# State-space scan: the entering states written beside B instead of into the scan's buffer

## The chip, the cores and the metric

The kernel runs on one core of one Trainium2 chip. The metric is the device time of one execution in microseconds (us). Engines are called as in the profile: PE (matrix products), DVE and POOL (elementwise work), ACT (activations and copies), SP (issues DMAs). Each engine works through its own queue in order; semaphores tie the queues together.

## The reference, cut to what matters

Two layers, each with a residual. The first is neighbourhood attention (7 x 7) on two images of 48 x 48 tokens with 768 channels. The second is a bidirectional selective scan over L = 2304 tokens, with 1536 inner channels d and 16 states n for each channel:

```python
def step(h, inp):
    d_t, B_t, C_t, u_t = inp
    dA = jnp.exp(d_t[..., None] * A)
    h = dA * h + (d_t * u_t)[..., None] * B_t[:, None, :]
    y = jnp.einsum('bdn,bn->bd', h, C_t)
    return (h, y)
```

`d_t` is delta (a softplus), `B_t` and `C_t` are rows of a small projection. The scan is run forward and backward with separate weights, `x * Dp` is added, the result is gated and projected, and everything is in fp32.

## The kernel before, in words

**Tiling.** Channels lie on partitions: 12 blocks `k` of 128. Time is cut into 6 chunks of `CL` = 384 tokens. A *pass* is one image, one direction and one chunk (24 passes); a *unit* is one channel block of a pass (288 units). A unit has four *groups* `g` of `SG` = 4 states, so there are 1152 groups. Within a chunk the recurrence over tokens is one instruction for two states: `tensor_tensor_scan` (line 1252) on a row of `W = CL + 2` = 386 cells per state.

**The two extra cells.** In the buffer `hb` of a group each state has 386 cells: 384 for the chunk, one ahead and one behind. The cell at the entering end holds the state that the previous chunk left; the one at the other end separates it from the next state. The decay tile `da` has fixed values, one and zero, in those two cells, set at the start of a pass direction (line 1188).

**One group** (`group` in `scan`) goes through these steps:
- `first` fills `hb`. It writes the eight end cells (the *edge fill*, lines 1216 or 1220), then the product of delta u and B over the 384 tokens of four states (line 1224). It runs whole on DVE or whole on POOL. On POOL it reads delta u from SBUF (`dus`), on DVE from a PSUM copy `du` that ACT makes once per unit (line 1193). `was` is the pair of state columns that go into the ends, or zeros in the first chunk.
- `step` on ACT makes exp(delta A), one instruction per state (line 1241), into one of two PSUM tiles `da`, each for two states.
- `two_steps` on DVE is the scan (line 1252).
- POOL multiplies by C (line 1267), ACT keeps the leaving state in `state` (line 1275), PE adds the states up by transposes (line 1284).

**Per three units** `deltas_of` loads `u` (line 1131 issues this load and that of the delta weights), makes delta on PE and ACT (lines 1142, 1148, 1153), `vt` = u Dp on ACT (line 1161), and delta u in place of `u` on POOL (line 1166).

**Per pass** `chunk` loads B and C, spread over all partitions, as four tiles each, `bc0` to `bc3` and `bc4` to `bc7` (line 1373). Each of the eight has one buffer, so a new chunk's load waits for the last reader of the old one.

**What sets the order.** Nothing is issued in source order. All work is handed to a planner (`Order`), with a price in ns, a key (the unit at which it is due), what it reads and writes, and sometimes an alternative engine (`alt`: three of the four groups may have `first` on the other engine). The planner plays the queues through with these prices and takes, for the engine that can start soonest, the work that is ready; with `early=EARLY` a work goes ahead of others that are ready then. It fixes the order in each queue once, and the program is built so. It also fills long waits of PE with transposes that change nothing (`idle`, line 1482). Beside the scans it places the rest: the first layer's attention of image 1, the input and output projections. Attention of image 0 comes ahead of all scans.

Of the kernel before, what the change touches and what calls it, by code (L numbers as in the profile page):

```python
# [16 lines left out]
P = 128  # L17
# [228 lines left out]
def tile_kernel(  # L246
# [34 lines left out]
    ]  # L281
    zero = res.tile([P, SG, 2], F32, tag="zero", name="zero")
    nc.gpsimd.memset(zero, 0.0)

    ones = wk.tile([1, CL], F32, tag="yt", name="ones", bufs=1)
    nc.gpsimd.memset(ones, 1.0)
# [32 lines left out]
    def sb(tag, shape, n, parts=1):  # L319
        return Buf(f"{tag}_{n}", wk, shape, tag, BUFS.get(tag, 1), parts)  # L320
# [26 lines left out]
    def act(n, pointers=0):  # L347
        return 60 + 90 * pointers + n * 0.833

    def dve(n):  # L350
        return 55 + n * 1.042

    def rows_of(t, k0, n, l0, cl):
        return t[k0 * P : (k0 + n) * P, l0 : l0 + cl].rearrange("(k p) l -> p k l", p=P)
# [768 lines left out]
    def deltas_of(ch, k0, x):  # L1123

        q, b, back, l0, cl, dt = (ch[v] for v in ("q", "b", "back", "l0", "cl", "dt"))
        c, at, n = slice(0, cl), x - 1.0, f"{ch['s']}_{k0}"
        u, w = sb("u", [P, KB, CL], n, KB), sb("dtw", [RK + 1, KB * P], n)
        dl = sb("dlt", [P, KB, CL], n, KB)

        def fetch():  # L1130
            nc.sync.dma_start(u[:, :, c], rows_of(us[back][b], k0, KB, l0, cl))
            nc.sync.dma_start(w.ap, q["dtT"][:, k0 * P : (k0 + KB) * P])

        add(
            "SP", 800, fetch, at - 0.7, r=[(us[back][b], cols(l0, cl, k0, KB))], w=[u, w],
            size=P * KB * (cl + RK) * 4,
        )
        for j in range(KB):
            acc = ps("mm", f"dl_{n}_{j}")
            add(  # L1140
                "PE", mm(1, cl),
                lambda j=j, acc=acc: nc.tensor.matmul(
                    acc[:, c], w[:, j * P : (j + 1) * P], dt[:, c], start=True, stop=True
                ),
                at + 0.01 * j, r=[dt, w, u], w=[acc, (dl, j)], early=EARLY,
            )
            add(
                "ACT", act(cl), lambda j=j, acc=acc: nc.scalar.copy(dl[:, j, c], acc[:, c]),
                at + 0.01 * j, [acc], [(dl, j)], early=EARLY,
            )  # L1150

        def softplus():
            nc.scalar.activation(dl[:, :, c], dl[:, :, c], AF.Softplus)
            nc.scalar.preload_act_table_set("natural_log_exp_and_others")

        add("ACT", 2600 + 120 + act(KB * cl), softplus, at + 0.05, [dl], [dl], early=EARLY)
        vts = [sb("vt", [P, CL], f"{n}_{j}") for j in range(KB)]
        for j in range(KB):
            add(
                "ACT", act(cl, 1) + 40,  # L1160
                lambda j=j: nc.scalar.mul(vts[j][:, c], u[:, j, c], q["Dp"][:, k0 + j : k0 + j + 1]),
                at + 0.03 + 0.25 * j, [(u, j)], [vts[j]], early=EARLY,
            )
            add(
                "POOL", 960,
                lambda j=j: nc.gpsimd.tensor_mul(u[:, j, c], dl[:, j, c], u[:, j, c]), at + 0.06 + 0.25 * j,  # L1166
                [(dl, j), (u, j)], [(u, j)], early=EARLY,
            )
        return [((dl, j), (u, j), vts[j]) for j in range(KB)]

    def scan(ch, k, x, dlj, duj, vt):
# [11 lines left out]
        if k == 0 and ch["first"]:  # L1183
# [6 lines left out]
                add("DVE", 200, turn, x - 0.1, w=[da])  # L1190
        du = ps("du", n)
        add(
            "ACT", act(cl), lambda: nc.scalar.copy(du[:, c], dus[:, ju, c]), x - 0.5, [duj], [du],
            early=EARLY,
        )

# [5 lines left out]
        def group(g):  # L1202
            m = f"{n}_{g}"
            now = at + 0.25 * g
            hb = sb("hb", [P, SG * W], m, SG + 1)
            body = (hb, range(SG))
            of = (slice(None), k, slice(g * SG, (g + 1) * SG))
            was = zero if ch["first"] else state[of][:, :, 0:2] if back else state[of][:, :, 1:3]

            def first():
                around = cells(hb, SG)[:, :, ends]
                if filled.eng == "POOL":
                    by, on = dus[:, ju, c], nc.gpsimd
                    on.tensor_copy(around, was)
                else:

                    by, on = du[:, c], nc.vector
                    on.scalar_tensor_tensor(  # L1220
                        around, du[:, : 2 * SG].rearrange("p (j e) -> p j e", e=2), 0.0, was, ALU.mult,
                        ALU.add,
                    )
                on.tensor_mul(  # L1224
                    cells(hb, SG)[:, :, h], by.unsqueeze(1).to_broadcast([P, SG, cl]), bc[g][:, :, c]
                )

            on = {"DVE": dve(SG * cl) + 75, "POOL": SG * cl * 2.2 + 140}
            main, other = ("DVE", "POOL") if g in (0, 1) else ("POOL", "DVE")
            filled = add(  # L1230
                main, on[main], first, now - (0.35 if main == "POOL" else 0.1),
                [du, duj, bc[g], (state, k * NSG + g)], [hb], after=marks.get(marks["n"] - 6),
                alt=(other, on[other]) if g in (1, 2, 3) else None,
            )

            def step(j):
                i = g * SG + j
                da = das[j // 2 % 2]
                add(
                    "ACT", act(cl, 1) + 45,  # L1240
                    lambda: nc.scalar.activation(  # L1241
                        cells(da, 2)[:, j % 2, h], dl[:, jd, c], AF.Exp, scale=q["A"][:, k, i : i + 1]
                    ),
                    now + 0.06 * j - 0.06, [dlj], [(da, j % 2)], due=True,
                )

            def two_steps(j):
                da = das[j // 2 % 2]
                at2 = (slice(None), slice(j * W, (j + 2) * W))
                mark = add(  # L1250
                    "DVE", (4 * W + 42) / 0.96,
                    lambda: nc.vector.tensor_tensor_scan(  # L1252
                        flip(hb[at2]), flip(da[:, : 2 * W]), flip(hb[at2]), 0.0, ALU.mult, ALU.add
                    ),
                    now + 0.06 * j, [da], [(hb, (j, j + 1, SG))],
                )
                marks[marks["n"]] = mark
                marks["n"] += 1

            for j in range(0, SG, 2):  # L1260
                step(j)
                step(j + 1)
                two_steps(j)

            add(
                "POOL", SG * cl * 2.03 + 10,
                lambda: nc.gpsimd.tensor_mul(  # L1267
                    cells(hb, SG)[:, :, h], cells(hb, SG)[:, :, h], bc[NSG + g][:, :, c]
                ),
                now + 0.25, [body, bc[NSG + g]], [body],  # L1270
            )
            if not ch["final"]:
                add(
                    "ACT", 90,
                    lambda: nc.scalar.copy(
                        state[of][:, :, 1:2], cells(hb, SG)[:, :, leaves : leaves + 1]
                    ),
                    now + 0.3, [body, (hb, SG)], [(state, k * NSG + g)],
                )

            def add_up():
                for j in range(SG):
                    for t in range(nt):
                        nc.tensor.matmul(  # L1284
                            py[:tp, t * P : (t + 1) * P], cells(hb, SG)[:, j, h][:, tb[t]], ident,
                            start=False,
                            stop=g == NSG - 1 and j == SG - 1 and t == nt - 1,
                            is_transpose=True, skip_group_check=True,
                        )

            add(
                "PE", SG * nt * 109 + 60, add_up, now + 0.45, [body, py], [py],
                opens=False if g == NSG - 1 else None,
            )
# [62 lines left out]
    def chunk(b, back, i, at):  # L1357
# [8 lines left out]
        )  # L1366
        bc = []
        for g in (0, 1, 2, NSG, 3, NSG + 1, NSG + 2, NSG + 3):
            t = sb(f"bc{g}", [P, SG, CL], s)
            r = RK + 1 + g * SG  # L1370
            add(
                "SP", 400,
                lambda t=t, r=r: nc.sync.dma_start(
                    t[:, :, :cl], src[r : r + SG, l0 : l0 + cl].partition_broadcast(P)
                ),
                at - 1 + 0.25 * (g % NSG) + 0.3 * (g >= NSG), [(src, cols(l0, cl))], [t],
                size=P * SG * cl * 4,
            )
            bc.append((g, t))
# [153 lines left out]
```

## Time and profile before

| what | value |
|---|---|
| time, median of 3 runs | 7284.69 us (7281.98 to 7290.29) |
| the profiled execution | 7284.3 us, its span 7282.5 us |
| DVE busy | 6207.4 us (85%) |
| POOL busy | 5628.0 us (77%) |
| ACT busy | 4924.7 us (68%) |
| PE busy | 6429.7 us (88%), of it fillers (L1482) 608.8 us |
| scans (L1252) | 2304, mean 1747 ns |
| `first` on DVE (L1224) / on POOL | 674, mean 1758 ns / 478, mean 3455 ns |
| product with C on POOL (L1267) | 1152, mean 3186 ns |
| exponentials (L1241) | 4608, mean 584 ns |
| edge fill on DVE (L1220) / on POOL (L1216) | 674, median 143 ns / 478, median 198 ns |
| state copy on ACT (L1275) | 960, mean 189 ns |

A line such as "L1252 DVE" is one source line on one engine. A wait is the time that an engine stood idle ahead of an instruction, put down to the instruction that released it. The name of a tile stands without buffer number, and `hb<-du,bc` means that `hb` is written from `du` and `bc`. [...]

### The profile page before, as it was taken

The numbers are of one execution on the slowest core, as the hardware profiler recorded it, in microseconds if no ns is written. First come the engines' busy times: TensorE is split into PE (matmuls) and PEld (weight loads), VectorE is DVE, ScalarE is ACT, GpSimd is POOL, SyncE is SP. The second block draws the span as 40 slices with busy tenths as digits, with TensorE's granted clock in tenths as the row PEclk, the third lists the DMA queues.
The fourth block names the chain that finished last, engine by engine and source line by source line (L and its number), as shares of the span: only waits on it lengthen the run. The fifth ranks groups of instructions, "written<-read, shape, count | busy, mean of one in ns | idle before, by whom it ended". The sixth has DMA issues, their size and how long they took to land.

```text
span 7282.5 us, 105644 instructions
## 1 busy us (share of the span) xinstructions
PE 6429.7 (88%) x38214; PEld 4891.8 (67%) x38214; DVE 6207.4 (85%) x7016; ACT 4924.7 (68%) x9948; POOL 5628.0 (77%) x2411
## 2 busy tenths in 40 slices
PE   7999988888899899899888888888888888889888
PEld 4555556666667766666666666666677887777777
DVE  1353449999888999888999999999999999999998
ACT  1232248788776787767888777778776666777764
POOL 0000009999988999869788899999999999999997
PEclk9999999999999999999999999999999999999999
DMA  6565453554556454554443542343466676555543
GB/s 180 169 198 154 138 162 102 157 151 127 153 163 189 137 158 137 157 166 135 134 144 94 157 141 91 100 133 110 132 178 188 170 204 201 181 165 170 168 147 107
DMA packets 1326322, 1101.03 MB, mean 151 GB/s; under 512 B 134168, under 2 KB 1316040, under 8 KB 1325768
## 3 DMA queue, kind: packets, MB, share of 16 engines
q1 hardware_dynamic: 1325800, 1094.27, 50.1%
q8 instruction: 303, 4.96, 0.3%
q14 instruction: 219, 1.79, 0.1%
HBM read 881.11 MB, written 213.57 MB: 150 GB/s over the span
## 4 chain that ended last, share of the span: by engine, by line
DVE 35%; PE 23%; POOL 15%; ACT 13%; issue 9%; DMA 4%; SPq 1%; DVEq 0%; POOLq 0%; ACTq 0%
DVE hb L1252 24%; POOL hb L1267 10%; POOL hb L1224 5%; DVE hb L1224 5%; PE mm_qk L382 5%; ACT da L1241 4%; DVE uz_u L931 3%; PE py L1284 3%; PE mm_v L382 2%; PE mm_ao L382 2%; PE mm_xin L382 1%; PE mm_z L382 1%; PE da L821 1%; ACT uz_u L924 1%; PE mm_out L382 1%
## 5 line engine op out<-in xcount | busy, mean ns | idle before, releaser
L1252 DVE TENSOR_TENSOR_SCAN hb<-da,hb 128x772 f32<-128x772 f32 x2304 | 3924.0, 1747 | 182.7 <-ACT da L1241 140.1
L1267 POOL TENSOR_TENSOR hb<-hb,bc 128x1536 f32<-128x1536 f32 x1152 | 3651.7, 3186 | 342.1 <-DVE hb L1252 286.0
L1241 ACT ACTIVATE da<-dlt,A 128x384 f32<-128x384 f32 x4608 | 2675.9, 584 | 1169.9 <-DVE hb L1252 1098.3
L1284 PE MATMUL py<-ident,hb 128*128 128x128 f32 x13824 | 1761.3, 281 | 263.8 <-POOL hb L1267 261.2
L1284 PEld LDWEIGHTS py<-ident,hb 128*128 128x128 f32 x13824 | 1591.2, 145 | 473.0 <-POOL hb L1267 366.7
L1224 POOL TENSOR_TENSOR hb<-u,bc 128x1536 f32<-128x1536 f32 x478 | 1651.7, 3455 | 38.6
L1224 DVE TENSOR_TENSOR hb<-du,bc 128x1536 f32<-128x1536 f32 x674 | 1184.7, 1758 | 23.0
L1166 POOL TENSOR_TENSOR u<-dlt,u 128x384 f32<-128x384 f32 x288 | 289.6, 1007 | 532.0 <-DMA bc<-xdf 412.9
L382 PE MATMUL mm_z<-xc,w_z 128*128 128x384 f32 x1728 | 609.9, 493 | 13.5 <-ACT uz_z L951 9.4
L1482 PE MATMUL py<-ident 128*128 128x128 f32 x4926 | 608.8, 278 | 0.0
L382 PE MATMUL mm_xin<-xc,w_x 128*128 128x390 f32 x1656 | 588.8, 498 | 21.3 <-DVE uz_u L931 8.5
L1482 PEld LDWEIGHTS py<-ident 128*128 128x128 f32 x4926 | 563.5, 143 | 25.2 <-issue 23.7
L382 PE MATMUL mm_out<-stage_y,w_o 128*128 128x192 f32 x3168 | 550.6, 331 | 15.2 <-DVE xr L1074 7.3
L382 PEld LDWEIGHTS mm_out<-stage_y,w_o 128*128 128x128 f32 x3168 | 522.1, 193 | 34.1 <-DVE xr L1074 9.3
L897 POOL MEMSET xc<- 128x18 f32 x4 | 0.5, 116 | 671.0 <-DMA dlt_qk<-in_w_qkv 671.0
L382 PEld LDWEIGHTS mm_xin<-xc,w_x 128*128 128x128 f32 x1656 | 309.3, 192 | 238.5 <-issue 23.4
L382 PEld LDWEIGHTS mm_z<-xc,w_z 128*128 128x128 f32 x1728 | 319.4, 192 | 220.6 <-ACT uz_z L951 16.5
L931 DVE SCALAR_TENSOR_TENSOR uz_u<-mm_xin,conv_w,uz_u 128x384 f32<-128x384 f32 x792 | 428.0, 607 | 36.0 <-ACT uz_u L924 32.8
L382 PE MATMUL mm_qk<-xc_xn,w_qk 128*128 128x384 f32 x1080 | 384.2, 501 | 11.7 <-ACT pT L828 2.9
L1300 PE MATMUL py<-ident,vt 128*128 128x128 f32 x864 | 160.4, 297 | 230.4 <-ACT yt L1310 230.1
L787 ACT ACTIVATE pr<-pr,sm 128x308 f32<-128x308 f32 x432 | 234.4, 543 | 134.7 <-DVE sm L781 134.2
L1300 PEld LDWEIGHTS py<-ident,vt 128*128 128x128 f32 x864 | 103.1, 148 | 295.0 <-ACT yt L1310 278.5
(171 smaller groups left out, 7043.4 us busy)
## 6 DMA issues: line engine op xcount, KB each, us to landing
w_o<-in_w_opT SPq DMA_DIRECT2D x264, 384.0 KB
bc<-xdf SPq DMA_DIRECT2D x96, 768.0 KB
bc<-xdb SPq DMA_DIRECT2D x96, 768.0 KB
w_x<-in_w_inT SPq DMA_DIRECT2D x144, 384.0 KB
w_z<-in_w_inT SPq DMA_DIRECT2D x144, 384.0 KB
w_qk<-in_w_qkv SPq DMA_DIRECT2D x108, 384.0 KB
u<-uf SPq DMA_DIRECT2D x48, 576.0 KB
sz<-uz_z SPq DMA_DIRECT2D x48, 576.0 KB
```

Of the source, the lines that this page charges most:

```text
L382: nc.tensor.matmul(acc[:m, o0 : o0 + cl], wb[:, wi, wo : wo + m], xb[:, xi, xo : xo + cl], start=c == 0, stop=c == n - 1,)
L787: nc.scalar.activation(pr[j].ap, pr[j].ap, AF.Exp, bias=sm[:, j : j + 1], scale=-1.0, accum_out=sm[:, 2 + j : 3 + j],)
L821: nc.tensor.transpose(bank(pt, 512 - P)[:nk, k * P : (k + 1) * P], pr[j][:, c0 : c0 + nk], ident,)
L931: nc.vector.scalar_tensor_tensor(u, px[:, at[j] : at[j] + cl], q["conv_w"][:, k, j : j + 1], u, ALU.mult, ALU.add,)
L1166: lambda j=j: nc.gpsimd.tensor_mul(u[:, j, c], dl[:, j, c], u[:, j, c]), at + 0.06 + 0.25 * j,
L1224: on.tensor_mul(cells(hb, SG)[:, :, h], by.unsqueeze(1).to_broadcast([P, SG, cl]), bc[g][:, :, c])
L1241: lambda: nc.scalar.activation(cells(da, 2)[:, j % 2, h], dl[:, jd, c], AF.Exp, scale=q["A"][:, k, i : i + 1]),
L1252: lambda: nc.vector.tensor_tensor_scan(flip(hb[at2]), flip(da[:, : 2 * W]), flip(hb[at2]), 0.0, ALU.mult, ALU.add),
L1267: lambda: nc.gpsimd.tensor_mul(cells(hb, SG)[:, :, h], cells(hb, SG)[:, :, h], bc[NSG + g][:, :, c]),
L1284: nc.tensor.matmul(py[:tp, t * P : (t + 1) * P], cells(hb, SG)[:, j, h][:, tb[t]], ident, start=False, stop=g == NSG - 1 and j == SG - 1 a ...
L1300: nc.tensor.matmul(py[:tp, t * P : (t + 1) * P], vt[:, tb[t]], ident, start=t == 0, stop=False, is_transpose=True, skip_group_check=True,)
L1482: nc.tensor.matmul(marks["py"][:, CL : CL + P], ident, ident, start=False, stop=False, is_transpose=True, skip_group_check=True,)
```

## The change

The edge fill of `first` goes. Instead:
- the tiles `bc0` to `bc3` get two more columns for each state, one ahead of B's 384 and one behind (`[P, SG, CL + 2]`); the load writes the middle, with rows of 1536 B now 4 B off the tile's start;
- for each group of a unit ACT copies the state pair `was` into those two columns (976 copies of 128 x 8 elements; in the first chunk of a direction only at `k == 0`, where they are zeros for the whole chunk);
- `u` also gets a column ahead and one behind; ACT writes ones into them once per load (96 copies), and delta u is made between them; `du` is copied with both;
- `first` is one product over 4 x 386 cells: one times state at the ends, delta u times B between.

The product with C, the scans, the exponentials and `bc4` to `bc7` stay. The planner's prices for `first` change from `dve(SG * cl) + 75` to `dve(SG * W)` on DVE and from `SG * cl * 2.2 + 140` to `SG * W * 2.2 + 20` on POOL, and all work is planned anew.

```diff
+    one = res.tile([P, KB, 2], F32, tag="one", name="one")
+    nc.gpsimd.memset(one, 1.0)
...
-        u, w = sb("u", [P, KB, CL], n, KB), sb("dtw", [RK + 1, KB * P], n)
+        u, w = sb("u", [P, KB, CL + 2], n, KB), sb("dtw", [RK + 1, KB * P], n)
...
-            nc.sync.dma_start(u[:, :, c], rows_of(us[back][b], k0, KB, l0, cl))
+            nc.sync.dma_start(u[:, :, h], rows_of(us[back][b], k0, KB, l0, cl))
...
+        add(
+            "ACT", 100, lambda: nc.scalar.copy(u[:, :, :: cl + 1], one), at - 0.3, w=[u], early=EARLY,
+        )
...
-                lambda j=j: nc.gpsimd.tensor_mul(u[:, j, c], dl[:, j, c], u[:, j, c]), at + 0.06 + 0.25 * j,
+                lambda j=j: nc.gpsimd.tensor_mul(u[:, j, h], dl[:, j, c], u[:, j, h]), at + 0.06 + 0.25 * j,
...
-            "ACT", act(cl), lambda: nc.scalar.copy(du[:, c], dus[:, ju, c]), x - 0.5, [duj], [du],
+            "ACT", act(cl), lambda: nc.scalar.copy(du[:, :W], dus[:, ju, :]), x - 0.5, [duj], [du],
...
-                around = cells(hb, SG)[:, :, ends]
-                if filled.eng == "POOL":
-                    by, on = dus[:, ju, c], nc.gpsimd
-                    on.tensor_copy(around, was)
-                else:
-
-                    by, on = du[:, c], nc.vector
-                    on.scalar_tensor_tensor(
-                        around, du[:, : 2 * SG].rearrange("p (j e) -> p j e", e=2), 0.0, was, ALU.mult,
-                        ALU.add,
-                    )
+                by, on = (dus[:, ju, :], nc.gpsimd) if filled.eng == "POOL" else (du[:, :W], nc.vector)
                 on.tensor_mul(
-                    cells(hb, SG)[:, :, h], by.unsqueeze(1).to_broadcast([P, SG, cl]), bc[g][:, :, c]
-                )
-
-            on = {"DVE": dve(SG * cl) + 75, "POOL": SG * cl * 2.2 + 140}
+                    cells(hb, SG), by.unsqueeze(1).to_broadcast([P, SG, W]), bc[g].ap
+                )
+
+            if k == 0 or not ch["first"]:
+                add(
+                    "ACT", 98, lambda: nc.scalar.copy(bc[g][:, :, ends], was), now - 0.4,
+                    [(state, k * NSG + g)], [(bc[g], 1)], early=EARLY,
+                )
+            on = {"DVE": dve(SG * W), "POOL": SG * W * 2.2 + 20}
...
-                [du, duj, bc[g], (state, k * NSG + g)], [hb], after=marks.get(marks["n"] - 6),
+                [du, duj, bc[g]], [hb], after=marks.get(marks["n"] - 6),
...
-            t = sb(f"bc{g}", [P, SG, CL], s)
+
+            o = int(g < NSG)
+            t = sb(f"bc{g}", [P, SG, CL + 2 * o], s, 1 + o)
...
-                    t[:, :, :cl], src[r : r + SG, l0 : l0 + cl].partition_broadcast(P)
+                    t[:, :, o : o + cl], src[r : r + SG, l0 : l0 + cl].partition_broadcast(P)
```

More of the change, by code (lines that the diff above doesn't have):

```diff
@@ L1125, in deltas_of @@
         q, b, back, l0, cl, dt = (ch[v] for v in ("q", "b", "back", "l0", "cl", "dt"))
-        c, at, n = slice(0, cl), x - 1.0, f"{ch['s']}_{k0}"
-        u, w = sb("u", [P, KB, CL], n, KB), sb("dtw", [RK + 1, KB * P], n)
+        c, h, at, n = slice(0, cl), slice(1, cl + 1), x - 1.0, f"{ch['s']}_{k0}"
+        u, w = sb("u", [P, KB, CL + 2], n, KB), sb("dtw", [RK + 1, KB * P], n)
         dl = sb("dlt", [P, KB, CL], n, KB)
         def fetch():
-            nc.sync.dma_start(u[:, :, c], rows_of(us[back][b], k0, KB, l0, cl))
+            nc.sync.dma_start(u[:, :, h], rows_of(us[back][b], k0, KB, l0, cl))
             nc.sync.dma_start(w.ap, q["dtT"][:, k0 * P : (k0 + KB) * P])
@@ L1160, in deltas_of @@
                 "ACT", act(cl, 1) + 40,
-                lambda j=j: nc.scalar.mul(vts[j][:, c], u[:, j, c], q["Dp"][:, k0 + j : k0 + j + 1]),
+                lambda j=j: nc.scalar.mul(vts[j][:, c], u[:, j, h], q["Dp"][:, k0 + j : k0 + j + 1]),
                 at + 0.03 + 0.25 * j, [(u, j)], [vts[j]], early=EARLY,
@@ L1372, in chunk @@
                 "SP", 400,
-                lambda t=t, r=r: nc.sync.dma_start(
-                    t[:, :, :cl], src[r : r + SG, l0 : l0 + cl].partition_broadcast(P)
+                lambda t=t, r=r, o=o: nc.sync.dma_start(
+                    t[:, :, o : o + cl], src[r : r + SG, l0 : l0 + cl].partition_broadcast(P)
                 ),
```

## The prediction

> **What bounds the kernel now.** I first read the page's busy shares, but over the whole span they mix two stages. So next comes the table by stretches:
>
> ```profile
> 0.00:1090.00 1090.00, 974.13 (x4589) 577.50 (x4590) 422.95 (x1506) 312.68 (x838) 5.47 (x15) 0.96 0.55 166
> ...
> 1700.00:2300.00 600.00, 526.19 (x2688) 386.09 (x2687) 510.06 (x451) 465.33 (x822) 523.63 (x230) 0.96 0.56 164
> ...
> 4700.00:5300.00 600.00, 523.37 (x3083) 403.77 (x3082) 574.59 (x517) 468.58 (x844) 568.73 (x248) 0.97 0.38 119
> ...
> 1090.00:7283.00 6193.00, 5455.56 (x33626) 4314.26 (x33624) 5784.48 (x5511) 4612.01 (x9110) 5622.50 (x2397) 0.97 0.50 148
> ```
>
> The busy columns are PE, PEld, DVE, ACT, POOL. The scan stage runs from 1090 us to the end and holds everything the change touches. In it DVE is busy 93% and POOL 91%; in a stretch without attention beside it, 96% and 95%. ACT is at 74%. PE's 88% includes 609 us of filler transposes (line 1482). So DVE and POOL are saturated together. Second, the waits of that stage:
>
> ```profile
> ACT da L1241 <- DVE hb L1252: 1098.3, 1351, 5.7
> ...
> POOL hb L1267 <- DVE hb L1252: 286.0, 144, 9.7
> ...
> DVE hb L1252 <- ACT da L1241: 140.1, 99, 5.8
> ...
> ACT du L1193 <- DVE hb L1224: 58.0, 61, 2.8
> ```
>
> The columns are total us, times, longest us. The exponentials wait for the scans in 1351 cases; the scans wait for the exponentials in 99. DVE sets the pace and ACT has room, but not everywhere. The last row matters as a model: an ACT copy placed as early as its planner allows found its reader unfinished 61 times in 288. Third, the timeline, for what an edge fill costs in place:
>
> ```profile
> 3004.49 0.14 DVE L1220 SCALAR_TENSOR_TENSOR hb<-du,state 128x8 f32<-128x8 f32 x1
> 3004.66 1.76 DVE L1224 TENSOR_TENSOR hb<-du,bc 128x1536 f32<-128x1536 f32 x1
> ...
> 3006.34 6.74 DVE L1252 TENSOR_TENSOR_SCAN hb<-da,hb 128x772 f32<-128x772 f32 x4
> ```
> ```profile
> 4442.47 0.19 POOL L1216 COPY hb<-zero 128x8 f32<-128x8 f32 x1
> 4442.74 3.45 POOL L1224 TENSOR_TENSOR hb<-u,bc 128x1536 f32<-128x1536 f32 x1
> 4446.13 6.33 POOL L1267 TENSOR_TENSOR hb<-hb,bc 128x1536 f32<-128x1536 f32 x2
> ```
>
> The columns are start and duration in us. The scan starts 0.08 us before the multiply ends, but the multiply starts after the edge fill ended: the pair doesn't overlap, and the fill costs its whole start-to-start time. Over all pairs of the trace the median of that is 0.177 us on DVE (674 pairs) and 0.279 us on POOL (478).
>
> [...] so I price by start-to-start times. [...] the 128x4 state copy (line 1275) takes 189 ns here. [...] the state copies of the trace agree, with 0.102 us in the median to the next start. [...]
>
> **The change part by part.** Edge fills go: DVE 674 x 0.177 = 119 us, POOL 478 x 0.279 = 133 us.
>
> Multiplies grow from 1536 to 1544 elements. DVE: 539 ns for 384 elements (line 1347) and 1758 ns for 1536 give 1.06 ns each, so 673 x 8.5 ns = 6 us. POOL: 3455/1536 = 2.25 ns each, 479 x 18 ns = 9 us. The built order also moves one multiply from DVE to POOL (net; 293 of 1152 change engine): 2 us off DVE, 3 us onto POOL. **DVE net -115 us, POOL net -121 us.** The wider du copy costs 288 x 2 x 0.8 ns = 0.5 us.
>
> ACT gains 976 copies of states into B's end columns and 96 copies of ones: 1072 x 0.102 us = 109 us where they lie back to back, 1072 x 0.19 = 204 us where not. What covers it is ACT's idle time before the exponentials (1098 us). It covers 1351 of 2304 pairs; 953 have no cover. An even share there is 45 to 84 us of later exponentials. Most of these pairs still have the length of a multiply to spare, since only 99 stalls show. I take a quarter: **+16 us**; none to all is 0 to 84.
>
> The new waits are the dear part. Each state copy must wait until the multiply of the unit before has read those columns (411 copies wait for DVE, 366 for POOL directly in the built program), the first of a chunk also for B's load, the ones for u's load. Queued behind on ACT are the exponentials, and behind these the scans. To bound it, I set the new ACT order against the times of before. On DVE, 356 of 514 such multiplies lie so that the next exponentials would wait for a later scan anyway; 66 lie right ahead of a scan whose exponentials are queued behind the copy, at most a copy and two exponentials late (1.4 us): 92 us. On POOL I add 3.47 us per multiply queued behind the end of the C product ahead of it: 147 of 366 readers end after the exponentials' old start, 86 late enough to reach the scan, 191 us in sum. Loads, from issue to the last packet by bytes in queue order (6.3 us median for B): 18 first copies late by 39 us, and 16 of the ones by 38 us (two larger ones, 44 us, are pieces of order that moved). **Sum 360 us if every lateness counted once, 0 if none does.** Most can't: one stall shifts all engines, and the next copies of a cluster then find their readers done; and POOL, whose lag makes the largest term, gets 0.28 us back per multiply. I take an eighth, **45 us**.
>
> Transfers: the same 1536 B packets. [...] The u fetch is issued as before, but the delta matmuls are now planned behind its ones copy; they are a unit ahead, so this is nothing beyond the 38 us above. PE: 97 filler transposes fewer (0.278 us each, in gaps): nothing.
>
> Sum against the profiled execution (7284.3 us, span 7282.5 us): 7284 - 115 + 16 + 45 = 7230 us. That execution lies 0.4 us from the median of the runs, 7284.69 us.
>
> **The rivals.** *All of it arrives:* DVE saturated at 96% speaks for it, the new waits in ACT's queue against: 7284 - 115 = 7169 us, with the load term 7185. *ACT's queue loses it (slower):* the place is a state copy in front of the exponentials whose reader is a late POOL multiply. For it: 1008 of POOL's 1152 C products start without having waited for a scan, so POOL runs with a queue behind it and ACT, which so far hardly waits for POOL, is tied to it. Against: the du copies, placed likewise, cost 58 us for 288, and DVE waited 33.5 us for them. It decides once more than 99 us of the 360 passes, over a quarter; at 40% (144 us) the time is 7284 - 115 + 16 + 144 = 7329 us. *A wash:* POOL, not DVE, or PE's chain of transposes keeps the pace, and gain and stalls cancel: 7270 to 7299 us. That the edges aren't really moved is excluded: the built program has no edge instruction on DVE or POOL.
>
> **How the numbers follow.** Forecast near 7230 us (7195 to 7268): 0.43. All arrives (7165 to 7195): 0.13. Wash: 0.11. Slower: 0.33. A change of under 0.2% (15 us) can't be told from none for this kernel. Faster is the first two, 0.56. The range 7175 to 7345 leaves out the tip of the best case and the worst of the slow one; the forecast's own is 7195 to 7268.
>
> **What would show it.** Right: no small fills on DVE and POOL; 976 ACT copies of about 190 ns; their idle time before them together under 250 us; scans waiting for exponentials under 220 us, against 140; DVE's busy time in the scan stage down by about 100 us. Wrong: state copies with idle times of 1 us and more released by POOL's or DVE's multiplies, and scans waiting over 250 us for exponentials; or POOL idle growing by as much as its fills gave, which would mean another chain.

## The result, and the profile after

The changed kernel takes 7208.99 us (median), the kernel before 7283.33 us on the same chip: a ratio of 0.9897, with a 95% interval from 0.9879 to 0.9914. That is 74 us less; the forecast was 54 us less. All ratios below are to the kernel before, with such intervals, and a difference of two ratios is given in us of 7284.

First the table by stretches (busy time of PE, PEld, DVE, ACT, POOL), changed kernel, a stretch without attention and then the whole scan stage:

```profile
4700.00:5300.00 600.00, 530.13 (x3021) 412.39 (x3020) 568.87 (x454) 489.69 (x980) 547.84 (x195) 0.95 0.41 127
1090.00:7212.00 6122.00, 5464.47 (x33536) 4327.72 (x33534) 5678.21 (x4837) 4724.51 (x10184) 5397.81 (x1923) 0.96 0.50 150
```

Over the scan stage DVE has 106 us less work (5784 before), POOL 225 us less (5622), ACT 112 us more (4612). But DVE also stands idle longer: 6122 - 5678 = 444 us against 6193 - 5784 = 409 us. So 106 - 35 = 71 us of DVE's 106 reached the end of the stage.

The waits of that stage (total us, times, longest us) say who took the rest:

```profile
ACT da L1242 <- DVE hb L1253: 869.0, 1271, 4.1
POOL hb L1268 <- DVE hb L1253: 495.5, 276, 39.0
...
DVE hb L1253 <- ACT da L1242: 211.3, 141, 9.1
...
ACT bc L1226 <- DVE hb L1220: 70.1, 132, 3.2
...
ACT du L1199 <- DVE hb L1220: 58.1, 59, 9.6
...
ACT bc L1226 <- DMA bc<-xdb: 24.2, 26, 2.8
...
ACT bc L1226 <- POOL hb L1220: 17.1, 24, 2.0
...
ACT bc L1226 <- DMA bc<-xdf: 13.9, 12, 2.9
```

The scans wait 211 us for exponentials, 71 us more than before. ACT stands 125 us in front of the new copies (line 1226), mostly until a DVE multiply is done (70 us) or B's load has landed (38 us), and little for POOL (17 us). POOL waits 495 us for scans where it waited 286 us: much of the time that it was given back became idle time.

In place, DVE goes from multiply to scan without a fill, and POOL from product to multiply (start and duration in us):

```profile
4439.40 1.75 DVE L1220 TENSOR_TENSOR hb<-du,bc 128x1544 f32<-128x1544 f32 x1
4441.08 6.72 DVE L1253 TENSOR_TENSOR_SCAN hb<-da,hb 128x772 f32<-128x772 f32 x4
```
```profile
4441.83 3.17 POOL L1220 TENSOR_TENSOR hb<-u,bc 128x1544 f32<-128x1544 f32 x1
4444.98 3.19 POOL L1268 TENSOR_TENSOR hb<-hb,bc 128x1536 f32<-128x1536 f32 x1
```

POOL's multiply takes 3.20 us in the mean, where 3.45 us plus eight elements were forecast. The copies themselves (below: minimum, median and maximum in ns) are as forecast, and the next instruction starts 0.103 us after one in the median:

```profile
L1226 ACT COPY bc<-state x960: 181/198/223, 1349.3 to 7151.3; 128x8 f32<-128x8 f32 x192
```

### The profile page after: what moved, and what is told of

It reads as the page before. It is cut to its first block, busy times and chain, and to the rows that moved or that the text cites. A ratio compares the mean times of both kernels' runs of the same rounds, so it can differ in the third digit from the quotient of the medians.

```text
span 7211.6 us, 105798 instructions
## 1 busy us (share of the span) xinstructions
PE 6439.9 (89%) x38117; PEld 4905.1 (68%) x38117; DVE 6101.1 (85%) x6341; ACT 5035.1 (70%) x11020; POOL 5400.7 (75%) x1935
## 4 chain that ended last, share of the span: by engine, by line
DVE 38%; PE 26%; ACT 17%; issue 8%; DMA 6%; POOL 4%; SPq 1%; DVEq 0%; POOLq 0%; ACTq 0%
DVE hb L1253 26%; DVE hb L1220 7%; ACT da L1242 5%; PE mm_qk L384 4%; DVE uz_u L933 3%; PE py L1285 3%; POOL hb L1268 3%; PE mm_ao L384 3%; PE mm_v L384 2%; PE mm_xin L384 2%; PE mm_z L384 2%; PE mm_out L384 2%; DMA bc<-xdb 2%; PE mm_dl L1148 1%; PE da L823 1%
## 5 line engine op out<-in xcount | busy, mean ns | idle before, releaser
L1285 PEld LDWEIGHTS py<-ident,hb 128*128 128x128 f32 x13824 | 1610.5, 146 | 345.4 <-POOL hb L1268 241.4
L1220 POOL TENSOR_TENSOR hb<-u,bc 128x1544 f32<-128x1544 f32 x479 | 1532.5, 3201 | 15.6 <-PE py L1285 15.0
L1220 DVE TENSOR_TENSOR hb<-du,bc 128x1544 f32<-128x1544 f32 x673 | 1169.4, 1743 | 74.8 <-PE py L1285 42.2
L1172 POOL TENSOR_TENSOR u<-dlt,u 128x384 f32<-128x384 f32 x288 | 263.3, 916 | 521.8 <-ACT dlt L1159 418.3
```

The costliest lines, as they stand in the source:

```text
L1172: lambda j=j: nc.gpsimd.tensor_mul(u[:, j, h], dl[:, j, c], u[:, j, h]), at + 0.06 + 0.25 * j,
L1220: on.tensor_mul(cells(hb, SG), by.unsqueeze(1).to_broadcast([P, SG, W]), bc[g].ap)
L1285: nc.tensor.matmul(py[:tp, t * P : (t + 1) * P], cells(hb, SG)[:, j, h][:, tb[t]], ident, start=False, stop=g == NSG - 1 and j == SG - 1 a ...
```

## The experiments

Two questions were open. Which parts of the change are worth what, with every queue's order held fixed? And what does a new order alone do, since the planner reorders all work when a price changes?

**Both fills put back, order of the changed kernel.**

```diff
+                around = cells(hb, SG)[:, :, ends]
+                if filled.eng == "POOL":
+                    on.tensor_copy(around, was)
+                else:
+                    on.scalar_tensor_tensor(
+                        around, du[:, : 2 * SG].rearrange("p (j e) -> p j e", e=2), 0.0, was, ALU.mult,
+                        ALU.add,
+                    )
                 on.tensor_mul(
```

> The changed kernel with the old edge fills put back in front of each wide multiply (674-odd small operations on DVE and POOL that the multiply then overwrites); every queue otherwise in the changed kernel's order. DVE theory (the fills' time on DVE is what was gained): 673 x 0.177 us come back, 7209 + 105 to 125 = 7314 to 7334 us. Rival (the gain came from the new order and a faster POOL multiply, and a fill is worth little): 7209 to 7260 us.

Measured: 1.0024 (1.0014 to 1.0033), that is 0.0127 x 7284 = 93 us over the changed kernel. That is far above the rival's range (51 us at most) and below the DVE theory's (105 to 125 us): the gain lies in the fills, but not all of their time arrives. More was put back than the 119 us counted. In this run a fill takes 0.181 us to the start of its multiply, and the multiply behind it 1.683 us to the next start, where it takes 1.663 us in the changed kernel (medians): 673 x 0.201 = 135 us.

**The fills on DVE alone put back.** The same edit, without POOL's branch.

> The changed kernel with the edge fills put back on DVE only (673, about 0.177 us each, overwritten by the multiply; all queues otherwise in the changed kernel's order). Both fills back cost 96 us. If DVE alone sets the pace: 80 to 96 us over the changed kernel, 7289 to 7305 us by the runs' ratio to before. If POOL's fills are half of it: 40 to 60 us over, 7250 to 7270 us.

Measured: 1.0023 (1.0014 to 1.0033), as with both, and within the range for DVE alone (the 96 us of the expectation is the difference of two medians from different chips). So POOL's 479 fills are worth nothing that these runs can show, though each takes 0.28 us, 134 us in all; the two intervals leave room for some 10 us. The scan-stage row of the run with both fills, and then of the run with DVE's alone:

```profile
1090.00:7290.00 6200.00, 5458.32 (x33478) 4313.05 (x33476) 5783.40 (x5502) 4728.83 (x10171) 5472.03 (x2395) 0.97 0.49 148
```
```profile
1090.00:7303.00 6213.00, 5495.44 (x33516) 4354.98 (x33514) 5784.81 (x5507) 4729.23 (x10175) 5394.01 (x1920) 0.96 0.49 148
```

DVE's 5783 and 5785 us of work go with one time, while POOL's differ by 78 us.

**The state copies left out**, for all blocks but the first of a pass; order unchanged.

```diff
-"ACT", 98, lambda: nc.scalar.copy(bc[g][:, :, ends], was), now - 0.4,
+"ACT", 98, (lambda: nc.scalar.copy(bc[g][:, :, ends], was)) if k == 0 else (lambda: None), now - 0.4,
```

> The changed kernel without the ACT copies of entering states for all blocks but the first of a pass (880 of 976 left out, so the states that enter are the wrong ones; all else and every queue's order unchanged). If ACT's copies and their waits eat the missing part of DVE's 120 us, as forecast (16 + 45 us): 7209 - 40 to -70 = 7139 to 7169 us. Rival (the copies are free, the rest went elsewhere): 7195 to 7215 us.

Measured: 0.9865 (0.9850 to 0.9879), 23 us under the changed kernel, with some 17 us of uncertainty from the two intervals. The copies aren't free, and they cost less than the forecast's 40 to 70 us: the value lies between the two ranges. This is the price of 880 copies. The 96 that stayed are the ones behind B's loads, and all of the waiting for these loads is still there (us, times):

```profile
DMA bc<-xdb: 26.0, 25
DMA bc<-xdf: 13.2, 11
```

No run takes it out. The scans of this run still wait for exponentials almost as long as in the changed kernel:

```profile
DVE hb L1253 <- ACT da L1242: 202.9, 140, 6.3
```

So most of the growth of that wait, from 140 to 211 us, is not the copies' doing. Nor is it due to the missing fills, since with both fills back it is still there:

```profile
DVE hb L1261 <- ACT da L1250: 189.9, 126, 8.0
```

By elimination it belongs to the new order; no run tests that alone.

**u shifted by one element, in the kernel before.** Nothing else changes, and all queues stand as before.

```diff
-        u, w = sb("u", [P, KB, CL], n, KB), sb("dtw", [RK + 1, KB * P], n)
+        u, w = sb("u", [P, KB, CL + 2], n, KB), sb("dtw", [RK + 1, KB * P], n)
...
-            nc.sync.dma_start(u[:, :, c], rows_of(us[back][b], k0, KB, l0, cl))
+            nc.sync.dma_start(u[:, :, h], rows_of(us[back][b], k0, KB, l0, cl))
```

The same `h` in place of `c` stands wherever u is read or written.

> The kernel before with one thing changed: rows of u are 386 wide and u lies one element into each row (no ones, fills as before, all queues in the order of before). If this shift is what made POOL's small multiply 0.09 us shorter, it takes 0.92 us here; POOL's wide multiply then shows whether its 0.25 us come from u's place too (3.20 us) or from the contiguous output (3.45 us). Time: DVE theory, 7283 within 15 us whatever POOL does; rival (POOL sets the pace too), up to 0.25 x 478 + 0.09 x 288 = 145 us less if both get shorter, 26 us less if only the small one does.

Measured: 0.9987 (0.9978 to 0.9996), 9 us less. POOL's multiplies in this run:

```profile
L1224 POOL TENSOR_TENSOR hb<-u,bc x478: 2900/3452/3502, 1087.3 to 7221.9; 128x1536 f32<-128x1536 f32 x160
```
```profile
L1166 POOL TENSOR_TENSOR u<-dlt,u x288: 853/872/1027, 1084.5 to 7174.6; 128x384 f32<-128x384 f32 x144
```

The small multiply takes 0.915 us in the mean, as expected. Neither expectation on the wide one fits: it takes 3.45 us for most and 2.90 us for a third (the hardware section says which). The scan-stage row:

```profile
1090.00:7274.00 6184.00, 5471.70 (x33621) 4335.27 (x33619) 5785.10 (x5510) 4609.85 (x9109) 5506.43 (x2397) 0.97 0.50 149
```

POOL has 116 us less work here than in the kernel before (5506 against 5622 us), and the time falls by 9 us, within the DVE theory's 15. POOL does not set the pace.

**What these runs don't hold fixed** is the clock that PE was granted. Its mean over the runs is 0.9675 in the kernel before (on the chip of the first experiment), 0.9642 in the changed kernel, 0.9616 with both fills back, 0.9595 with DVE's alone, 0.9642 without the copies and 0.9647 with u shifted. Among the runs of one kernel, where there are ten or more, a clock lower by 0.001 goes with some 3 to 5 us more; whether it makes them, no run shows. If it does, some 8 to 13 of the 93 us belong to the clock, POOL's fills may be worth up to some 20 us, and the shift of u some 17 to 23 us in place of 9 (estimates from these figures). Which engine sets the pace stays the same; the sizes are less sharp.

**New orders alone.** These runs change only the planner's prices of `first`, in ns, and so the order of all queues; no instruction changes in kind.

```diff
-on = {"DVE": dve(SG * cl) + 75, "POOL": SG * cl * 2.2 + 140}
+on = {"DVE": dve(SG * cl) + 197, "POOL": SG * cl * 2.2 + 310}
```

> The kernel before with its planner's prices for first set to the measured start-to-start times with fill (DVE +197 in place of +75, POOL +310 in place of +140), so all work is planned anew and no instruction changes. DVE theory: the order as such is worth little, 7283 within 25 us. Rival (better prices, and so a better order, made the gain): 7210 to 7240 us.

> The kernel before with the measured price for first on DVE alone (+197 in place of +75; POOL's stays +140). If a true price of DVE, which sets the pace, makes the better order: 7215 to 7245 us, most of the gain of both prices. If luck makes it: anything from 7200 to 7310 us, with no relation to the run that has both prices.

> The kernel before with 4 ns added to both planner prices of first (+79 and +144): the same question for the order of before. If its order is only one of many equal ones: 7288 within 10 us. If it was an unlucky one: 7215 to 7270 us, and the 0.98% of the run with measured prices is not due to their being right.

> The kernel before with the measured prices plus 4 ns each (+201 and +314 in place of +197 and +310): a third order from prices that are as true. If true prices make the order good: 7205 to 7230 us again. If the 0.98% was luck: back among the other orders of before, 7245 to 7285 us.

> The changed kernel with 4 ns added to both planner prices of first, which no trace would call wrong: a new order of all queues, no other instruction. It measures what a new order alone moves. If orders made from prices this close are worth the same: 7209 within 10 us. If the order is luck: 7209 with 20 us or more to either side, and then a good part of the changed kernel's 74 us can be luck too.

| instructions of | prices of first (DVE, POOL) | ratio, 95% interval |
|---|---|---|
| before | +75, +140 (as it is) | 1 |
| before | +79, +144 | 0.9965 (0.9952 to 0.9978) |
| before | +197, +140 | 0.9994 (0.9986 to 1.0003) |
| before | +197, +310 (measured) | 0.9902 (0.9885 to 0.9918) |
| before | +201, +314 | 0.9947 (0.9932 to 0.9962) |
| changed | +0, +20 (as it is) | 0.9897 (0.9879 to 0.9914) |
| changed | +4, +24 | 0.9921 (0.9904 to 0.9938) |

This was the surprise. One new order of the old instructions is as fast as the changed kernel, in the rival's range (7212 us by the ratio). But 4 ns on each price undoes almost half of that (33 us) and lands in the range named for luck (7245 us). DVE's price alone gains nothing (7279 us). And 4 ns moves the kernel before by 25 us, as named for an unlucky order, and the changed one by 17 us, between its two expectations and no more than the two intervals allow by chance. So an order is worth some 20 to 30 us by luck, and single runs of replanned kernels can't be compared more finely. A place where it shows is the stretch from 3100 to 3400 us, in the kernel before and then in the one with 4 ns more:

```profile
3100.00:3400.00 300.00, 276.26 (x1714) 203.85 (x1714) 253.48 (x290) 219.78 (x529) 245.40 (x105) 0.97 0.49 151
```
```profile
3100.00:3400.00 300.00, 279.40 (x1851) 215.80 (x1852) 277.19 (x298) 227.49 (x536) 275.62 (x117) 0.98 0.49 153
```

DVE does 24 us more work in the second. In the first its longest waits are for the attention's output product on PE, and in the second this wait is not among those of the stretch:

```profile
DVE xr_x L707 <- PE mm_ao L382: 19.8, 5, 7.5
```

**POOL's prices set to the trace, in the changed kernel.**

```diff
-"POOL": SG * W * 2.2 + 20}
+"POOL": SG * W * 2.03 + 25}
```

(the small multiply of u from 960 to 830; the second run has 4 ns more on both prices of `first`)

> The changed kernel with the planner's POOL prices set to what its trace shows: first to 3.16 us (was 3.42), the small multiply of u to 0.83 us (was 0.96). Theory that true prices make better orders: a gain, 7150 to 7195 us, some multiplies moving from DVE to POOL. Rival (DVE's price was true already and POOL, with 12% idle, doesn't matter): 7195 to 7225 us.

> The changed kernel with POOL's measured prices, plus 4 ns on both prices of first. If measured POOL prices are worth something: again under the changed kernel, 7180 to 7205 us. If luck: 7205 to 7240 us.

Measured: 0.9870 (0.9853 to 0.9886) and 0.9896 (0.9881 to 0.9912). Multiplies do move to POOL (507 in the first run, 479 in the changed kernel). The first gains 20 us, in the range named for true prices, the second 1 us, in that for luck; with the luck of an order as large as that, a gain is not shown.

**The same prices, and the copies without precedence.**

```diff
-                    [(state, k * NSG + g)], [(bc[g], 1)], early=EARLY,
+                    [(state, k * NSG + g)], [(bc[g], 1)],
```

> The changed kernel with POOL's measured prices, and the 976 state copies without their precedence in ACT's queue, so that each is planned when nothing older is ready. If the copies' idle time (125 us, most of it released by DVE's multiplies) reaches the scans, this wins back part of the 23 us that the copies cost: 7165 to 7190 us. Rival (a copy put later holds up the multiply that needs it): 7200 to 7240 us.

Measured: 0.9860 (0.9843 to 0.9877), 7183 us, in the range expected: the lowest of all, 27 us under the changed kernel and clear of its interval, but only 7 us under the run with the same prices, which the intervals don't tell apart. 523 multiplies run on POOL, and the scans wait less:

```profile
DVE hb L1253 <- ACT da L1242: 168.5, 122, 5.7
```

Its copies still wait 60 us for DVE's multiplies, so it isn't shown that their place helped.

## Why the prediction was right, and where it was not

**The bound.** "DVE and POOL are saturated together" was wrong for POOL. Busy at 91%, it still doesn't set the pace: 116 us taken off it by the shift of u gave 9 us, and its fills gave nothing that can be told from none. The sign I had named for another chain (POOL idle growing by as much as its fills gave) appeared: idle time before the C product grew from 342 to 572 us. Here it meant no new chain: POOL spent the time that it got back waiting for scans, DVE's own work. The signs for being right showed too: 976 copies with a median of 198 ns and 125 us of waits before them (under 250), scans waiting 211 us (under 220), DVE's busy time down by 106 us. Of the other sign for being wrong, 15 copies did wait 1 us or more for a multiply, but the scans stayed under its 250 us.

**DVE's term, -115 us,** has the right mechanism and was near as work: fill and multiply took 0.177 + 1.675 = 1.852 us from start to start (medians), the wide multiply 1.663 us, so 673 x 0.189 = 127 us went. The forecast let the multiply grow by 8.5 ns, and it shrank by 12 (the last section has the two forms side by side). But the forecast let all of it arrive: of some 135 us put back at a fixed order, 93 us did (69%).

**POOL's term, -121 us,** was half of what happened (-225 us of busy time): the multiply got shorter, not longer, and so did the small multiply of u (1007 to 916 ns), at which the forecast had nothing. It had no weight in the sum.

**ACT's terms, 16 + 45 us,** were too large as far as they were measured: 23 us for the work and waits of 880 copies. The first copies of each pass and the 96 copies of ones are not in this; they waited 38 us for B's loads, near the 39 us of the bound, and 7 us for u's, against 38 us, and what that cost is not measured. The wider `du` copy was as forecast: 478.0 ns in the mean against 476.2, 0.5 us in all. The wait for POOL was the largest part of the bound (191 of 360 us) and came to 17 us of ACT's idle time in 24 waits, against 147 readers counted late; it was counted with POOL's old durations. On DVE 132 copies waited, 70 us in all, where 66 costly ones and 92 us were counted. The quarter and the eighth that the forecast took of its bounds had no run behind them.

**The sum.** At a fixed order it is -93 + 23 = -70 us, against -74 us measured and -54 us forecast. Against these figures ACT's terms were 38 us too large and DVE's 22 us, and the two errors partly cancel: that the forecast came this near is in part luck.

**The missing term** is the order. The prediction counted 293 multiplies that change engine and took the new order at nothing. For this pair that holds within the noise: the changed kernel with both fills back runs at 1.0024, and less the copies' 0.0032 that leaves 0.9992 for the old work in the new order, but with POOL's faster multiplies, if the two add up. That is 6 us less than before, with some 18 us to either side from the three intervals. But a term with 20 to 30 us to either side belonged in the range. The rival with all of it arriving and the slower one fell by the fixed-order runs: 93 us arrived of 135, and the 880 copies cost 23 us, not 99 or more. The wash fell with the result itself.

**What stays open.** Of five orders of the old instructions none is slower than the one on record (one is level with it); the two from measured prices are the two fastest (0.9902 and 0.9947). True prices may make better orders, and part of what the fills cost might then be had without the change. Two such orders, 33 us apart from each other, don't settle it. In the mean of the five old orders (0.9962) and of the four new ones with precedence (0.9896) the new instructions are 48 us faster, not 74. And fills put back into an order that was planned without them may cost another amount than in an order planned for them. That all four orders with the new instructions and precedence (0.9870 to 0.9921) lie under four of the five old ones agrees with the fixed-order result.

## What to carry to other kernels

Price a removed instruction by its start-to-start time, with what it adds to the one behind it (0.181 + 0.020 us here for a DVE fill of 0.147 us), on the engine that sets the pace, and find that engine by adding or removing work on one engine at a fixed order, not by its busy share: 93% and 91% looked alike here, and one was worth some 70% of its time and the other less than a tenth as measured (some fifth with the clock's part added). Where a planner or scheduler decides the order, measure a few orders from prices that differ by nothing that matters before crediting an edit with its gain. Small work moved into another engine's queue has to be measured with what it holds up there: here 880 copies, with some 87 of ACT's 125 us of waiting in front of the new copies, cost at most some 40 us of the kernel's time.

## What the runs showed of the hardware that was not expected

POOL's two-input multiply took different times for the same work with u at another place within 16 bytes: 2.90 or 3.45 us for the wide one, 0.87 or 1.01 us for the small one. The three blocks of a load of u lie in rows of 1544 B once u is shifted, so the middle one lies 8 B off the others within 16 B, while the first and third, 3088 B apart, lie alike. With u shifted and nothing else changed, the wide multiply takes 2.90 us for the middle block, where u starts 12 B past a 16 B line (by the built program's addresses), and 3.45 us for the two that start 4 B past one; in the kernel before, with u on a line, it takes 3.45 us. All of these write four rows of 384, which start 4 and 12 B past a line by turns, and read B on a line. In the changed kernel, one contiguous row of 1544 on a line with u 0 or 8 B past one takes 3.20 us. The small multiply, in place, takes 1.01 us with all three on a line, 0.87 us with u 4 B past it, and 1.01 us again with u 12 B past it. What in the hardware does this was not tested.

DVE's multiply has one row in place of four and eight elements more, and takes less. It isn't the row: with the fills put back, the same one-row multiply takes longer again (the changed kernel, then both fills back; the mean in ns stands after the busy time):

```profile
L1220 DVE TENSOR_TENSOR hb<-du,bc 128x1544 f32<-128x1544 f32 x673 | 1169.4, 1743 | 74.8 <-PE py L1285 42.2
L1228 DVE TENSOR_TENSOR hb<-du,bc 128x1544 f32<-128x1544 f32 x673 | 1189.1, 1767 | 23.7 <-DVE hb L1224 0.2
```

Behind a fill the multiply waits for DVE's own semaphore and starts 0.034 us after the fill's end (kernel before); without one it starts 0.081 us before the end of its predecessor (changed kernel; medians). So a fill, 0.147 us long with both put back, cost more than its own time: 0.181 us to the start of its multiply, and 0.020 us in the multiply.

The trace shows no dearer packet where B's rows lie 4 B off: a 1536 B packet takes 75 ns in the mean before and after, though a quarter of these packets write shifted rows after. From issue to last packet, in queue order, a load of B takes 6.3 us in the median before and 6.5 us after.
